# A recommender's CIN layer on one core: weights gathered in two halves, from the input and from a smaller table

## The chip, the cores and the metric

The kernel runs on one core of one Trainium2 chip. The metric is the device time of one execution in microseconds (us). A profile of one execution goes with it. In it PE is TensorE (matmuls; PEld are its weight loads), DVE is VectorE, ACT is ScalarE, POOL is GpSimd and SP is SyncE. "L391" is line 391 of the kernel. A fp32 matmul leaves two records, so 8 records of line 391 are 4 matmuls.

## The reference

Three layers combine an embedding `X0` of 1024 rows, 39 fields and 64 elements with itself; each is summed over the elements, and a last linear layer takes the 192 sums to one number for each row:

```python
F, E, HID = 39, 64, [64, 64, 64]
def _cin_layer(Xk, X0, W, b):
    O = W.shape[0]
    Hk, Fdim = (Xk.shape[1], X0.shape[1])
    Wr = W.reshape(O, Hk, Fdim)
    return jnp.einsum('bhe,bfe,ohf->boe', Xk, X0, Wr) + b[None, :, None]
Xk = X0; outs = []
for W, b in ((W0, b0), (W1, b1), (W2, b2)):
    Xk = _cin_layer(Xk, X0, W, b)
    outs.append(Xk.sum(axis=-1))
return jnp.concatenate(outs, axis=-1) @ fc_w.T + fc_b
```

All data are fp32. The last layer only enters through its sum, so the kernel folds fc into W2 (a vector v), and v into W1: a table T[b, a, h]. What is left for each pair of fields is one product of two embeddings, a weight from W0 for the first layer's output x1, and a weight from T for a second output z; the answer is the sum over x1 * (z + fc) and a linear part.

## The kernel before

A start-up of some 33 us makes the table and gathers weights. Then come 32 blocks of 32 rows. For a block, four "rolled" tiles `r` (the 39 fields in four orders, gathered by GpSimd from a copy `xd` of the input) give six products `p` of 128 field pairs each (chunks 0 to 5), and for each pair of blocks the tiles `u` and `v` give one more product for the rest (chunk 6, half the rows for each block). TensorE multiplies each product with that chunk's weights `wa`. The weights of both orders of a pair, (a, b) and (b, a), are gathered into `wa` and `wb` and added.

The table has x1's half (W0) and z's half (T) side by side, 512 bytes a row; unused pairs point at a row of zeros:

```python
NONE = FT * FT - 1                     # FT = F + 1 = 40
table = dram.tile([FT * FT, 2 * H], F32, name="table")
...                                    # start-up: loads and memsets
load(0, nc.gpsimd)
nc.gpsimd.memset(w0s, 0.0); nc.gpsimd.memset(w0r, 0.0)     # (two lines)
load(1, nc.gpsimd)
...
halves(w2s, w2); halves(w1s, w1)                            # SyncE's queue
nc.scalar.dma_start(fc, fc_w.rearrange("o (l h) -> h (o l)", h=H))
load_ones(0, nc.scalar)
nc.scalar.copy(warm, warm)
for k in range(2):
    nc.scalar.dma_start(w0s[H * k : H * k + F], w0t[:, NA * k : NA * (k + 1), :])
nc.scalar.dma_start(w0r[0:F], w0t[:, 2 * NA : F, :])
for s in range(2):
    nc.scalar.copy(fc2[H * s : H * s + H, 0:1], fc[:, 2:3])
    nc.scalar.copy(v2[H * s : H * s + H, F:FT], fc[:, 1:2])
...                                    # VectorE works out the lists of indices
roll(0, (0, 1, 2))
roll(1, (0, 1))
...                                    # pv matmuls (fc into W2), transposes, v2; more lists
...                                    # pt and pr matmuls (v into W1)
spin(9)                                # filler matmuls on zeros
for s, copy in enumerate((nc.vector.tensor_copy, nc.scalar.copy)):
    ...                                # PSUM to part and rest
nc.sync.dma_start(tablev[:, 0:NA, :], part[0:FT])
nc.scalar.dma_start(tablev[:, NA : 2 * NA, :], part[H : H + FT])
nc.sync.dma_start(tablev[:, 2 * NA : FT, :], rest[0:FT])

def weights(c):                        # two gathers of 128 rows of 512 bytes
    for k, w in enumerate((wa, wb)):
        nc.gpsimd.indirect_dma_start(
            w[:, c], None, table[:], bass.IndirectOffsetOnAxis(ap=wlists[:, k, c : c + 1], axis=0)
        )

weights(0); weights(1); weights(3)     # (one call a line in the kernel)
roll(1, (2,))
weights(2)
roll(0, (3,))
weights(4); weights(5)
roll_half(0)                           # u and v
weights(6)
roll(1, (3,))
load(2); load(3)
```

The main loop, and the order of its steps:

```python
PAIRS = ((0, 1), (0, 2), (0, 3), (1, 2), (2, 3), (1, 3)); ORDER = (0, 1, 3, 2, 4, 5)
steps = [(n, c) for n in range(2) for c in ORDER[:3]]
steps += [(0, c) for c in ORDER[3:] + (NPAIR,)] + [(1, c) for c in ORDER[3:]]
for n in range(2, NBLK, 2):
    steps += [(n, c) for c in ORDER + (NPAIR,)] + [(n + 1, c) for c in ORDER]
...
p = {s: product(*s) for s in steps[:2]}
add(steps[0][1])
p[steps[2]] = product(*steps[2])
add(steps[1][1]); add(steps[2][1])     # (one a line)
p[steps[3]] = product(*steps[3])
for at, (n, c) in enumerate(steps[:-TAIL]):
    if c == 0 and n + 4 < NBLK:
        load(n + 4)
    add(steps[at + 2][1])              # VectorE: wa += wb, once for each chunk
    multiply(n, c, p.pop((n, c)))      # TensorE: 4 matmuls (8 half-height ones for chunk 6)
    if at - 1 in over:
        finish(over[at - 1]); fields(over[at - 1] + 1)
    if at + AHEAD < len(steps):        # AHEAD = 4
        n, c = steps[at + AHEAD]
        p[n, c] = product(n, c)        # VectorE
        if c == ORDER[-1] and n + 2 < NBLK:
            roll(n + 2)
            ...                        # and u, v of the next pair of blocks
```

There are four buffers for `p`.

Of the kernel before, what the change touches and what calls it, by code (L numbers as in the profile page):

```python
# [49 lines left out]
F32 = mybir.dt.float32  # L52
I32 = mybir.dt.int32
AF = mybir.ActivationFunctionType
ALU = mybir.AluOpType
# [3 lines left out]
FH = F * H  # L59
# [20 lines left out]
FT = F + 1  # L80
NONE = FT * FT - 1
NTAB = 3
# [13 lines left out]
def cin_kernel(ctx: ExitStack, tc: tile.TileContext, x, w0t, b0, w1, b1, w2, b2, fc_w, fc_b, out):  # L96
# [16 lines left out]
    def load(n, engine=nc.sync):  # L113
        first = n % 2 * FT
        engine.dma_start(
            xd[n // 2 % NTAB][first : first + F].rearrange("f (b e) -> f b e", e=E),
            xv[:, n * BB : (n + 1) * BB, :],
        )
# [7 lines left out]
    def roll(n, tiles=range(4)):  # L126
        for i in tiles:
            gather_rows(rt[n % 2][:, i], n, n % 2 * 4 + i)
# [20 lines left out]

    table = dram.tile([FT * FT, 2 * H], F32, name="table")  # L150
    tablev = table.rearrange("(b a) h -> b a h", a=FT)

    prep = tc.tile_pool(name="prep", bufs=1)
    with prep as prep:
        w2s = prep.tile([128, FH // 2], F32, name="w2s")
        w1s = prep.tile([128, FH // 2], F32, name="w1s")
        fc2 = prep.tile([128, 32], F32, name="fc2")
        ones = prep.tile([16, 128], F32, name="ones")
        zeros = prep.tile([128, MM], F32, name="zeros")
        w0s = prep.tile([128, NA * H], F32, name="w0s")  # L160
        w0r = prep.tile([H, NR * H], F32, name="w0r")
        part = prep.tile([128, NA, 2 * H], F32, name="part")
        rest = prep.tile([H, NR + 1, 2 * H], F32, name="rest")
        place = prep.tile([128, 1], I32, name="place")
        warm = prep.tile([1, 1], F32, name="warm")


        nc.gpsimd.iota(place, pattern=[[0, 1]], base=0, channel_multiplier=1)
        nc.vector.memset(warm, 0.0)
        nc.vector.memset(zeros, 0.0)  # L170
        nc.vector.memset(fc2, 0.0)  # L171
        nc.vector.memset(ones, 1.0)
        load(0, nc.gpsimd)
        nc.gpsimd.memset(w0s, 0.0)
        nc.gpsimd.memset(w0r, 0.0)
        load(1, nc.gpsimd)
        nc.gpsimd.memset(v2, 0.0)
        nc.gpsimd.memset(rest[:, NR], 0.0)

        def halves(dst, w):  # L180
            for s in range(2):
                nc.sync.dma_start(
                    dst[H * s : H * s + H], w[:, s * (FH // 2) : (s + 1) * (FH // 2)]
                )

        def load_ones(k, engine):
            for row in (F, FT + F):
                engine.dma_start(xd[k][row].rearrange("(p c) -> p c", c=128), ones)

        halves(w2s, w2)  # L190
        halves(w1s, w1)
        nc.scalar.dma_start(fc, fc_w.rearrange("o (l h) -> h (o l)", h=H))
        load_ones(0, nc.scalar)
        nc.scalar.copy(warm, warm)
        for k in range(2):
            nc.scalar.dma_start(w0s[H * k : H * k + F], w0t[:, NA * k : NA * (k + 1), :])
        nc.scalar.dma_start(w0r[0:F], w0t[:, 2 * NA : F, :])
        for s in range(2):
            nc.scalar.copy(fc2[H * s : H * s + H, 0:1], fc[:, 2:3])  # L199
            nc.scalar.copy(v2[H * s : H * s + H, F:FT], fc[:, 1:2])  # L200
# [52 lines left out]
        nc.vector.tensor_scalar(lists[:, 4:8], fields_of[:, 0:4], float(FT), None, ALU.add)  # L253
        roll(0, (0, 1, 2))
        roll(1, (0, 1))

        step(row, HR, 1.0, half)
        fused(q, half, -float(HR), row, ALU.mult, ALU.add)
        nc.vector.tensor_tensor(field[4], q, step(q, F, -float(F)), ALU.add)
        nc.vector.tensor_tensor(field[4], field[4], step(q, 56, 11.0), ALU.add)  # L260
        nc.vector.tensor_scalar(field[5], q, float(F), None, ALU.min)
        fused(t, q, -50.0, step(q, 45, 1.0), ALU.add, ALU.mult)
        for y in (t, step(q, 50, -float(F)), step(q, 56, -6.0)):
            nc.vector.tensor_tensor(field[5], field[5], y, ALU.add)

        nc.vector.tensor_scalar(half, half, float(FT), None, ALU.mult)
        nc.vector.tensor_scalar(lists[:, 8:10], fields_of[:, 4:6], half, None, ALU.add)

# [5 lines left out]
        for k in range(2):  # L274
            for u in range(4):
                rows = slice(u % 2 * H, u % 2 * H + H)
                f0 = u // 2 * 19 + k * 10
                nc.tensor.matmul(  # L278
                    pv[k][32 * u : 32 * u + 32, 0:320],
                    fc2[rows],  # L280
                    w2v[rows, f0 : f0 + 10, :],
                    start=True,
                    stop=True,
                )
# [9 lines left out]
        nc.scalar.copy(v2[H:128, 0:F], column)  # L294
        nc.scalar.copy(part[:, :, H : 2 * H], w0s.rearrange("b (a h) -> b a h", h=H))
        nc.scalar.copy(rest[:, 0:NR, H : 2 * H], w0r.rearrange("b (a h) -> b a h", h=H))


        nc.vector.tensor_scalar(scaled, fields_of, float(FT), None, ALU.mult)
        pair = prep.tile([128, 4], F32, name="pair")  # L300
        nc.vector.tensor_scalar(wlists[:, 0, 0:3], scaled[:, 1:4], field[0], None, ALU.add)
        nc.vector.tensor_scalar(wlists[:, 1, 0:3], fields_of[:, 1:4], scaled[:, 0:1], None, ALU.add)
        nc.vector.tensor_tensor(wlists[:, 0, 3:5], scaled[:, 2:4], fields_of[:, 1:3], ALU.add)
        nc.vector.tensor_tensor(wlists[:, 1, 3:5], scaled[:, 1:3], fields_of[:, 2:4], ALU.add)
        for m, (i, k) in enumerate(((1, 3), (3, 1), (4, 5), (5, 4))):
            nc.vector.tensor_tensor(pair[:, m : m + 1], scaled[:, k : k + 1], field[i], ALU.add)
        fused(wlists[:, 0, 5:6], extra, float(NONE), pair[:, 0:1], ALU.mult, ALU.max)
        fused(wlists[:, 1, 5:6], extra, float(NONE), pair[:, 1:2], ALU.mult, ALU.max)
        last = step(q, 62, float(NONE))
        nc.vector.tensor_tensor(wlists[:, 0, 6:7], pair[:, 2:3], last, ALU.max)  # L310
        nc.vector.tensor_scalar(t, q, float(F), float(NONE), ALU.is_lt, ALU.mult)
        nc.vector.tensor_tensor(pair[:, 3:4], pair[:, 3:4], t, ALU.max)
        nc.vector.tensor_tensor(wlists[:, 1, 6:7], pair[:, 3:4], last, ALU.max)

# [14 lines left out]
        for s in range(2):  # L329
# [3 lines left out]
            )  # L333
        spin(9)
        for s, copy in enumerate((nc.vector.tensor_copy, nc.scalar.copy)):
            at = slice(32 * s, 32 * s + 32)
            copy(part[:, :, at], pt[s].rearrange("b (a h) -> b a h", h=32))
            copy(
                rest[:, 0:NR, at],
                pr[s][H * s : H * s + H, 0 : 32 * NR].rearrange("b (a h) -> b a h", h=32),  # L340
            )
        nc.sync.dma_start(tablev[:, 0:NA, :], part[0:FT])
        nc.scalar.dma_start(tablev[:, NA : 2 * NA, :], part[H : H + FT])
        nc.sync.dma_start(tablev[:, 2 * NA : FT, :], rest[0:FT])
        for k in range(1, NTAB):
            load_ones(k, nc.scalar)


    def weights(c):
        for k, w in enumerate((wa, wb)):  # L350
            nc.gpsimd.indirect_dma_start(  # L351
                w[:, c], None, table[:], bass.IndirectOffsetOnAxis(ap=wlists[:, k, c : c + 1], axis=0)
            )

    weights(0)
    weights(1)
    weights(3)
    roll(1, (2,))
    weights(2)
    roll(0, (3,))  # L360
    weights(4)
    weights(5)
    roll_half(0)
    weights(6)
    roll(1, (3,))
# [16 lines left out]
    def multiply(n, c, p, quarters=range(BLK // MM)):  # L382
        half = c == NPAIR
        for k in (n, n + 1) if half else (n,):
            if k not in po:
                po[k] = [bank("po") for _ in range(BLK // MM)]
        for m in quarters:

            for h in range(2 if half else 1):
                w = slice(h * HR, (h + 1) * HR) if half else slice(0, 128)  # L390
                nc.tensor.matmul(  # L391
                    po[n + h][m],
                    wa[w, c, :],
                    p[w, bass.ts(m, MM)],
                    start=c == opens[n + h],
                    stop=c == closes[n + h],
                )
# [47 lines left out]

    def add(c):
        nc.vector.tensor_tensor(wa[:, c], wa[:, c], wb[:, c], ALU.add)

    AHEAD = 4
# [14 lines left out]
    last_weights()  # L464
    p = {s: product(*s) for s in steps[:2]}
    added = set()
# [6 lines left out]
    add(steps[0][1])  # L473
    p[steps[2]] = product(*steps[2])
    add(steps[1][1])
    add(steps[2][1])
    p[steps[3]] = product(*steps[3])
    fields(0)
# [76 lines left out]
```

## Time and profile before

| what | value |
|---|---|
| time, median of 3 runs | 767.87 us (766.59 to 769.39) |
| profiled span | 766.5 us, mean TensorE clock 0.991 |
| main matmuls, first start | 33.13 us |
| W2 and W1 issued on SyncE's queue | 0.74 and 1.99 us |
| first matmul on W2 (pv) | 9.77 us |
| last table issue | 17.49 us |
| first gather from the table | 28.36 us |

The page gives each engine's busy time as a share of the span; a line of the waits reads "engine, line <- releaser: us in all, times, the longest". A line of the timeline reads start, duration, engine, line, operation, output <- inputs with shapes, how many were merged, and in brackets the idle time ahead of it and what ended it. A gather's duration on POOL is that of its issue; the data land later. A wait for several events is put down to the one that came last.

### The profile page before, as it was taken

The numbers are of one execution on the slowest core, as the hardware profiler recorded it, in microseconds if no ns is written. First come the engines' busy times: TensorE is split into PE (matmuls) and PEld (weight loads), VectorE is DVE, ScalarE is ACT, GpSimd is POOL, SyncE is SP. The second block draws the span as 40 slices with busy tenths as digits, with TensorE's granted clock in tenths as the row PEclk, the third lists the DMA queues.
The fourth block names the chain that finished last, engine by engine and source line by source line (L and its number), as shares of the span: only waits on it lengthen the run. The fifth ranks groups of instructions, "written<-read, shape, count | busy, mean of one in ns | idle before, by whom it ended". The sixth has DMA issues, their size and how long they took to land.

```text
span 766.5 us, 5146 instructions
## 1 busy us (share of the span) xinstructions
PE 745.1 (97%) x1856; PEld 322.3 (42%) x1856; DVE 641.2 (84%) x479; ACT 160.4 (21%) x207; POOL 320.4 (42%) x185
## 2 busy tenths in 40 slices
PE   6597999999999999999999999999999999999998
PEld 2243444444444444444444444444444444444443
DVE  5375988889888889888889988888988888998885
ACT  2002312122221212222121222112122221112212
POOL 4487273542436244253634325363442636334200
PEclk9899999999999999999999999999999999999999
DMA  8849958576865757676575777657577764737400
GB/s 260 268 151 384 402 183 342 168 273 231 327 240 203 283 170 276 244 316 241 189 287 183 276 254 292 256 178 284 185 297 252 267 260 147 284 150 317 165 0 0
DMA packets 62839, 181.79 MB, mean 237 GB/s; under 512 B 41364, under 2 KB 41499, under 8 KB 42254
## 3 DMA queue, kind: packets, MB, share of 16 engines
q0 software_dynamic: 23712, 169.34, 57.5%
q1 hardware_dynamic: 38494, 11.36, 6.4%
q10 hardware_dynamic: 608, 0.77, 0.3%
q8 instruction: 14, 0.23, 0.1%
q14 instruction: 11, 0.09, 0.0%
HBM read 180.58 MB, written 11.10 MB: 250 GB/s over the span
## 4 chain that ended last, share of the span: by engine, by line
PE 91%; DMA 3%; issue 2%; POOL 2%; DVE 1%; ACT 0%; DVEq 0%; POOLq 0%; SPq 0%
PE po L391 91%; DMA table<-rest 1%; POOL wa L351 1%; DMA u<-xd,lists 1%; POOL wb L351 1%; DMA wb<-table,wlists 0%; PE pt L322 0%; DVE blocks L289 0%; POOL r L122 0%; DVE fields_of L233 0%; DVE tmp L229 0%; DVE tmp L233 0%; PE pr L331 0%; DVE g L430 0%; DVE sums L432 0%
## 5 line engine op out<-in xcount | busy, mean ns | idle before, releaser
L391 PE MATMUL po<-p,wa 128*128 128x512 f32 (+1 forms) x1792 | 724.3, 597 | 11.9 <-DVE wa L471 11.9
L377 DVE TENSOR_TENSOR p<-r 128x2048 f32<-128x2048 f32 x192 | 434.5, 2291 | 88.1 <-PE po L391 82.2
L391 PEld LDWEIGHTS po<-p,wa 128*128 128x128 f32 (+1 forms) x1792 | 315.0, 190 | 420.4 <-issue 395.4
L122 POOL DMA_INDIRECT r<-xd,lists x128 | 249.3, 1948 | 366.0 <-DVE p L377 340.0
L410 ACT ACTIVATE x<-po,b0s 64x512 f32<-64x512 f32 x124 | 84.5, 684 | 356.4 <-PE po L391 349.8
L404 ACT COPY g<-u 39x1024 f32<-39x1024 f32 x64 | 66.6, 1043 | 216.2 <-DVE sums L421 181.2
L416 DVE SCALAR_TENSOR_TENSOR g<-po,fc,x 64x512 f32<-64x512 f32 x124 | 86.4, 734 | 0.0
L421 DVE TENSOR_REDUCE sums<-g 103x16 f32<-103x1024 f32 x62 | 75.6, 1220 | 2.2
L379 DVE TENSOR_TENSOR p<-u,v 128x2048 f32<-128x2048 f32 x16 | 36.5, 2284 | 9.1 <-DMA v<-xd,lists 9.1
L122 POOL DMA_INDIRECT u<-xd,lists x16 | 29.8, 1859 | 4.9 <-issue 4.6
L122 POOL DMA_INDIRECT v<-xd,lists x16 | 16.6, 1035 | 4.9 <-issue 4.9
L351 POOL DMA_INDIRECT wa<-table,wlists x7 | 11.0, 1573 | 14.6 <-DMA table<-rest 12.8
L211 PE MATMUL idle<-zeros 128*128 128x512 f32 x24 | 12.9, 686 | 1.5 <-DVE fc L171 1.5
L471 DVE TENSOR_TENSOR wa<-wa,wb 128x128 f32<-128x128 f32 x7 | 2.0, 291 | 11.6 <-DMA wb<-table,wlists 11.6
L351 POOL DMA_INDIRECT wb<-table,wlists x7 | 9.7, 1382 | 2.1 <-issue 2.1
L211 PEld LDWEIGHTS idle<-zeros 128*128 128x128 f32 x24 | 4.8, 212 | 8.2 <-issue 6.8
L430 DVE SCALAR_TENSOR_TENSOR g<-po,fc,x1q 64x512 f32<-64x512 f32 x4 | 3.0, 742 | 5.3 <-ACT x1q L429 5.3
L278 PE MATMUL pv<-w2s,fc 64*32 64x320 f32 x16 | 2.8, 764 | 4.5 <-ACT fc L199 4.5
L289 DVE STREAM_TRANSPOSE blocks<-pv 64x320 f32<-64x320 f32 x4 | 2.1, 514 | 3.7 <-issue 3.6
L429 ACT ACTIVATE x1q<-po,b0s 64x512 f32<-64x512 f32 x4 | 2.7, 684 | 10.2 <-PE po L391 10.2
L278 PEld LDWEIGHTS pv<-w2s,fc 64*32 64x32 f32 x16 | 1.0, 142 | 6.7 <-ACT fc L199 6.1
L432 DVE TENSOR_REDUCE sums<-g 103x8 f32<-103x512 f32 x4 | 2.7, 686 | 0.1
(74 smaller groups left out, 30.0 us busy)
## 6 DMA issues: line engine op xcount, KB each, us to landing
xd<-in_x SPq DMA_DIRECT2D x30, 312.0 KB
r<-xd,lists POOLq DMA_INDIRECT x128
w2s<-in_w SPq DMA_DIRECT2D x2, 312.0 KB
xd<-in_x POOLq DMA_DIRECT2D x2, 312.0 KB
w1s<-in_w SPq DMA_DIRECT2D x2, 312.0 KB
table<-part SPq DMA_DIRECT2D x1, 320.0 KB
table<-part ACTq DMA_DIRECT2D x1, 320.0 KB
w0s<-in_w0t ACTq DMA_DIRECT2D x2, 156.0 KB
```

The source lines that it names most:

```text
L122: nc.gpsimd.indirect_dma_start(dst, None, table, bass.IndirectOffsetOnAxis(ap=lists[:, k : k + 1], axis=0))
L211: nc.tensor.matmul(idle, zeros[:, 0:128], zeros, start=True, stop=True)
L278: nc.tensor.matmul(pv[k][32 * u : 32 * u + 32, 0:320], fc2[rows], w2v[rows, f0 : f0 + 10, :], start=True, stop=True,)
L351: nc.gpsimd.indirect_dma_start(w[:, c], None, table[:], bass.IndirectOffsetOnAxis(ap=wlists[:, k, c : c + 1], axis=0))
L377: nc.vector.tensor_tensor(p, rt[n % 2][:, i], rt[n % 2][:, k], ALU.mult)
L379: nc.vector.tensor_tensor(p, ut[n // 2 % 2], vt[n // 2 % 2], ALU.mult)
L391: nc.tensor.matmul(po[n + h][m], wa[w, c, :], p[w, bass.ts(m, MM)], start=c == opens[n + h], stop=c == closes[n + h],)
L404: nc.scalar.copy(gt[H : H + F], ut[n // 2 % 2][h : h + F, bass.ts(m, SUB)])
L410: nc.scalar.activation(x1[m // 2][:, bass.ts(m % 2, MM)], po[n][m][H:128], AF.Identity, bias=b0s[H:128])
L416: nc.vector.scalar_tensor_tensor(gt[0:H, at], po[n][m][0:H], fc[:, 0:1], x1[m // 2][:, at], ALU.add, ALU.mult)
L421: nc.vector.tensor_reduce(sums[:, b_at : b_at + SB], gt.rearrange("p (b e) -> p b e", e=E), AX.X, ALU.add)
L430: nc.vector.scalar_tensor_tensor(gt[0:H], po[n][m][0:H], fc[:, 0:1], t, ALU.add, ALU.mult)
```

## The change

W0's half of the weights is no longer copied into the table: it is gathered from the input itself. The table keeps T alone, with rows of 256 bytes. Each chunk now takes four gathers of 128 rows of 256 bytes instead of two of 512. Rows beyond the source are skipped instead of pointing at zeros, so `wa` and `wb` are cleared first. W2 is loaded first and as one transfer, with fc's column going straight to where pv's matmuls read it. Two of block 0's tiles are issued ahead of the table's way through the engines and a third just ahead of the table's gathers; block 1's load and tiles come after the first table gathers. The purpose is to have the table, and with it the first main matmul, earlier, and to use GpSimd while it waits for the table.

The core of the diff (cut at "..."):

```diff
-NONE = FT * FT - 1
+NONE = 4096
...
-    table = dram.tile([FT * FT, 2 * H], F32, name="table")
-    tablev = table.rearrange("(b a) h -> b a h", a=FT)
+    table = dram.tile([FT * F, H], F32, name="table")
+    tablev = table.rearrange("(b a) h -> b a h", a=F)
+
+    def weights(c, into, of, last):
+        for k in range(2):
+            nc.gpsimd.indirect_dma_start(
+                (wa, wb)[k][:, c, into : into + H],
+                None,
+                of,
+                bass.IndirectOffsetOnAxis(ap=wlists[:, k, c : c + 1], axis=0),
+                bounds_check=last,
+                oob_is_err=False,
+            )
+
+    def weights_x1(c):
+        weights(c, H, w0t.rearrange("b a h -> (b a) h"), F * F - 1)
+
+    def weights_z(c):
+        weights(c, 0, table[:], FT * F - 1)
...
+        for t in (wa, wb):
+            nc.gpsimd.memset(t, 0.0)
...
-        load(0, nc.gpsimd)
-        nc.gpsimd.memset(w0s, 0.0)
-        nc.gpsimd.memset(w0r, 0.0)
-        load(1, nc.gpsimd)
...
-        halves(w2s, w2)
-        halves(w1s, w1)
-        nc.scalar.dma_start(fc, fc_w.rearrange("o (l h) -> h (o l)", h=H))
+        fcv = fc_w.rearrange("o (l h) -> h (o l)", h=H)
+        nc.sync.dma_start(w2s, w2.rearrange("o (s n) -> (o s) n", s=2))
+        for s in range(2):
+            nc.scalar.dma_start(fc2[s:128:2, 32 * s : 32 * s + 1], fcv[:, 2:3])
+        load(0)
+        nc.scalar.dma_start(fc, fcv)
+        nc.sync.dma_start(w1s[0:H], w1[:, 0 : FH // 2])
         load_ones(0, nc.scalar)
+        nc.scalar.dma_start(w1s[H:128], w1[:, FH // 2 : FH])
         nc.scalar.copy(warm, warm)
-        for k in range(2):
-            nc.scalar.dma_start(w0s[H * k : H * k + F], w0t[:, NA * k : NA * (k + 1), :])
-        nc.scalar.dma_start(w0r[0:F], w0t[:, 2 * NA : F, :])
...
-        roll(0, (0, 1, 2))
-        roll(1, (0, 1))
...                                      # (some index arithmetic moves ahead, some behind the table)
+        weights_x1(0)
+        roll(0, (0,))
+        weights_x1(1)
+        roll(0, (1,))
...                                      # (pv's matmuls: all 128 rows of W2 at once)
+        weights_x1(3)
...
-        spin(9)
+        spin(13)
...
-    weights(0)
-    weights(1)
-    weights(3)
-    roll(1, (2,))
-    weights(2)
+    roll(0, (2,))
+    weights_z(0)
+    weights_z(1)
+    load(1, nc.gpsimd)
+    weights_z(3)
+    roll(1, (0, 1, 2))
+    weights_x1(2)
+    weights_z(2)
     roll(0, (3,))
-    weights(4)
-    weights(5)
+    weights_x1(4)
+    weights_z(4)
     roll_half(0)
-    weights(6)
+    weights_x1(5)
+    weights_z(5)
+    weights_x1(6)
+    weights_z(6)
     roll(1, (3,))
...
-    p = {s: product(*s) for s in steps[:2]}
+    p = {steps[0]: product(*steps[0])}
...
     add(steps[0][1])
-    p[steps[2]] = product(*steps[2])
-    add(steps[1][1])
-    add(steps[2][1])
-    p[steps[3]] = product(*steps[3])
+    for k in (1, 2, 3):
+        p[steps[k]] = product(*steps[k])
+        if k < 3:
+            add(steps[k][1])
```

## The prediction

> **What bounds the kernel now.** I read the page's engine list first, then the waits, then the chain, then the first 75 us of the timeline engine by engine.
>
> ```profile
> PE 745.1 (97%) x1856; PEld 322.3 (42%) x1856; DVE 641.2 (84%) x479; ACT 160.4 (21%) x207; POOL 320.4 (42%) x185
> ```
>
> TensorE is the bound over the whole run. The waits say where it is not fed:
>
> ```profile
> PE po L391 <- DVE wa L471: 11.9, 2, 7.8
> PE pv L278 <- ACT fc L199: 4.5, 1, 4.5
> ```
>
> So the main loop waits twice, both times for a weight sum (the add of line 471). The TensorE timeline dates them:
>
> ```profile
> 33.13 29.25 PE L391 MATMUL po<-p,wa 128*128 128x512 f32 x64 [7.85 <-DVE wa L471]
> 66.44 9.03 PE L391 MATMUL po<-p,wa 128*128 128x512 f32 x24 [4.06 <-DVE wa L471]
> ```
>
> Eight steps (8 records each) run from 33.13, then there is a hole, and from 66.44 on there is no further wait. A warm step lasts 3.43 us (records start 0.429 us apart). Step 8 starts at 66.44, step 9 at 71.77, step 10 at 75.41 us, and from there the kernel needs 766.5 - 75.4 = 691.1 us, which the change leaves alone. So the whole question is: **when does step 10 start?** (Steps counted from 0, in the order of the list `steps`: step 8 is block 0 with weight chunk 5, step 9 the half-height chunk 6, step 10 block 1 with chunk 2.)
>
> What sets it is GpSimd, which issues every gather. From its timeline after the table has landed:
>
> ```profile
> 28.36 0.95 POOL L351 DMA_INDIRECT wa<-table,wlists  x1 [12.75 <-DMA table<-rest]
> 29.62 0.95 POOL L351 DMA_INDIRECT wb<-table,wlists  x1 [0.30 <-issue]
> ...
> 43.70 2.67 POOL L351 DMA_INDIRECT wa<-table,wlists  x1 [0.31 <-issue]
> 46.67 1.89 POOL L351 DMA_INDIRECT wb<-table,wlists  x1 [0.30 <-issue]
> 48.87 1.92 POOL L351 DMA_INDIRECT wa<-table,wlists  x1 [0.30 <-issue]
> 51.09 1.90 POOL L351 DMA_INDIRECT wb<-table,wlists  x1 [0.30 <-issue]
> ...
> 59.46 0.94 POOL L122 DMA_INDIRECT r<-xd,lists  x1 [0.31 <-issue]
> ```
>
> and VectorE at the same time:
>
> ```profile
> 43.26 8.92 DVE L377 TENSOR_TENSOR p<-r 128x2048 f32<-128x2048 f32 x4 [1.93 <-DMA r<-xd,lists]
> ...
> 63.89 2.29 DVE L379 TENSOR_TENSOR p<-u,v 128x2048 f32<-128x2048 f32 x1 [9.12 <-DMA v<-xd,lists]
> 66.10 0.28 DVE L471 TENSOR_TENSOR wa<-wa,wb 128x128 f32<-128x128 f32 x1
> 67.91 2.29 DVE L377 TENSOR_TENSOR p<-r 128x2048 f32<-128x2048 f32 x1 [1.52 <-DMA r<-xd,lists]
> 70.12 0.28 DVE L471 TENSOR_TENSOR wa<-wa,wb 128x128 f32<-128x128 f32 x1
> ```
>
> The reader is to see three things. An issue costs 0.95 us and 0.30 us of gap, 1.25 us, whether its rows have 512 or 8192 bytes. When it starts while VectorE multiplies it lasts about 2 us: it ends some 0.85 us after that product does. And VectorE is in order: the product of u and v stands ahead of the add for chunk 5, the product with block 1's field tile 3 ahead of the add for chunk 6, so TensorE's "wait for wa" is really a wait for v and for that tile, the last of GpSimd's list.
>
> **What the Trainium skill says.** "SBUF — State Buffer", section "SBUF: two separate sides", describes the lock: a DMA issued from GpSimd needs descriptors written by GpSimd, which cannot get at the shared port pair while certain VectorE instructions hold it. The trace agrees: 2.67, 1.89, 1.92, 1.90 us against 0.95. "DMA: Bandwidth & Descriptors", section "Anatomy of one DMA — SWDGE (gpsimd) path", gives a fixed cost of about 2 us per transfer, so splitting one gather in two saves nothing per piece. Here a weight gather issued at 36.30 was added at 38.82, 2.5 us, for 64 KB. "TensorE: Matmul & The Clock Gate", section "What's actually happening", says that an idle window of about 3.4 us halves the clock. Here the first records after both holes start about 0.86 us apart instead of 0.43; step 8 took 5.33 us, 1.9 more than a warm one.
>
> **The change part by part.** (1) The start. The copies of W0 through SBUF (on ScalarE) go, and W2's transfer is first and alone, with fc's column brought straight into place. TensorE's first useful matmul (pv) waited until 9.77 us for ScalarE's copy of fc, which stood behind the W0 transfers; I estimate 6 us. From there to the last table issue it was 17.76 - 9.77 = 8 us, so about 14 us. The table write then needed 10.15 us in the chain, behind five 1 MB gathers (DMA share near 1.0 from 5 to 25 us). Now only two 1 MB gathers are ahead, and the table is half as large: I estimate 4 us, landing at 18.
>
> (2) GpSimd ahead of the table. The lists are ready at about 6.5 us (5.8 before, plus five small VectorE operations). Six W0 gathers and three 1 MB gathers, 9 x 1.25, take it to 17.8. So the first table gather starts at about 18.5 instead of 28.36, and the first main matmul at about 24.5 instead of 33.13: 8.6 us **early**. The 13 filler matmuls (11.1 us, from about 13) end at the same time, so that TensorE is warm here, worth another 1.7 us. If nothing followed, this would give 757 to 759 us.
>
> (3) GpSimd behind it. Before, from the table's landing to block 1's tile 3, it issued 19 gathers: 14 of weights, 3 field tiles, u and v, from 28.36 to 60.40, 32.0 us. Of that 19 x 1.25 = 23.8, and 8.3 us are seven stretched issues, 1.2 us each. After, the same stretch has 14 table gathers, 8 of W0 (chunks 2, 4, 5, 6), the load of block 1, five field tiles (block 1's tiles 0 and 1, which went ahead of the table before, are now behind), u and v: **30 issues**. 30 x 1.25 = 37.5, and ten products fall into the stretch, 10 x 1.2 = 12: 49.5 us, so it ends at 68.0. Walked issue by issue, with each issue that starts in a product held to 0.87 us past its end, it ends nearer 70; the same walk on the old order gives step 9 at 71.5 and step 10 at 75.0, where the trace has 71.77 and 75.41. So 68 to 70 against 60.40.
>
> (4) What TensorE sees. v is issue 21 of the 30: 21 x 1.25 + 8 x 1.2 + 18.5 = 54.4 (57 in the walk), landing some 6.5 later, so step 8 starts at 64 to 66, about where it did. Then tile 3 of block 1: issued by 68 to 70, 4.8 us to its product (38.50 to 43.26 for its like), 2.29 of product, 0.3 of add: 75.4 to 77.7 for step 9, against 71.77. The hole ahead of it is near 8 us, so step 9 runs at half clock for 3.4 us, 1.7 more, and step 10 starts at 75.4 + 5.3 = 80.7 to 77.7 + 5.3 = 83.0, against 75.41: **5.3 to 7.6 us later**. The early start is eaten on the way: block 1's first product waits for its tiles until about 42.
>
> **The rivals.** Rival A: the early start survives (757 to 761). The filler count, raised from 9 to 13, looks like a start meant for 24 us. Against it: in the windows of 40:50 and 50:60 us GpSimd was already busy 8.7 and 8.2 of 10 us with half as many weight gathers. It could still come true in part if gathers of 256 bytes with skipped rows issue faster: at 0.85 instead of 0.95 us the walk puts step 10 at 79.1, 3.7 late; at 0.6 the two would about cancel. Rival B: the bounds test makes an issue dearer. No row of the old trace has such a gather. At 1.3 us the walk puts step 10 at 87, 779.6 in all. Rival C: the table is late after all, since transfers from SyncE's queue sat 3.7 us between issue and first packet when the queues were full; each microsecond past 18.5 is then a microsecond on the end, 2 to 3 us in all.
>
> **Range and chances.** The middle of the sum is 6.5 us on 767.87: 774.5. The low end, 764, is rival A by half; the high end, 782, is B or C. For 2% faster, 752.5, the whole start would have to be gained twice over. For 2% slower, 783.2, both B and C would have to hold, or a new hole open.
>
> **What would show it.** Right: first main matmul at 24 to 25 us; a second hole of several microseconds right ahead of the half-height step; GpSimd busy over 8 of 10 us from 20 to 70 us with issues of about 2 us beside products; step 10 past 80 us; no holes later. Wrong: table gathers of clearly less than 0.9 us or more than 1.1; products that no longer stretch them; step 10 at 75 or earlier; or any wait of TensorE beyond 90 us, which I take to be none.

## The result and the profile after

The changed kernel takes 776.5 us (median of 4 runs, 774.03 to 777.43), the kernel before 767.83 beside it: a ratio of 1.0107, 95% interval 1.0077 to 1.0137. The change costs some 8.7 us.

The page's engine list of the changed kernel (busy time, share of the span, instructions):

```profile
PE 751.8 (97%) x1864; PEld 324.1 (42%) x1864; DVE 641.5 (83%) x482; ACT 158.7 (20%) x203; POOL 338.4 (44%) x196
```

and its waits of TensorE:

```profile
PE po L406 <- DVE wa L483: 11.0, 3, 7.9
PE po L406 <- DVE p L392: 6.8, 1, 6.8
```

GpSimd works 18 us longer. The wait of pv for ScalarE has gone. TensorE in the main loop waited 11.9 us in all before, and now 17.8: 6.8 us for a product are new. The TensorE timeline dates the waits (start, duration, engine, line, operation, tiles, records; in brackets the idle time ahead):

```profile
5.17 3.65 PE L282 MATMUL pv<-w2s,fc 128*32 128x320 f32 x16
...
26.89 10.88 PE L406 MATMUL po<-p,wa 128*128 128x512 f32 x24 [1.34 <-DVE wa L483]
44.60 19.79 PE L406 MATMUL po<-p,wa 128*128 128x512 f32 x40 [6.83 <-DVE p L392]
66.18 3.70 PE L406 MATMUL po<-p,wa 128*128 128x512 f32 x8 [1.79 <-DVE wa L483]
77.75 22.62 PE L406 MATMUL po<-p,wa 64*128 64x512 f32 x53 [7.87 <-DVE wa L483]
```

The early start is there: 26.89 us instead of 33.13. It is gone at step 3, which starts at 44.60, about where it did before. Step 8 starts at 66.18 (before 66.44), step 9, the half-height one, at 77.75 (71.77), and step 10, read from the single records, at 84.22 (75.41). From there to the end it is 775.7 - 84.22 = 691.5 us, as before (691.1). So 8.8 of the 9.2 us between the two profiled spans are there when step 10 starts, and **all of them arise between step 8 and step 10**. Of the 8.8 us, 6.0 are the later start of step 9, and 2.8 are its length: it took 6.47 us where it took 3.64 before, at half clock after the hole.

Why step 9 is late is read from VectorE's timeline, back from its add:

```profile
22.58 2.29 DVE L392 TENSOR_TENSOR p<-r 128x2048 f32<-128x2048 f32 x1 [5.01 <-DMA r<-xd,lists]
26.50 0.29 DVE L483 TENSOR_TENSOR wa<-wa,wb 128x128 f32<-128x128 f32 x1 [1.63 <-DMA wb<-table,wlists]
...
42.26 2.29 DVE L392 TENSOR_TENSOR p<-r 128x2048 f32<-128x2048 f32 x1 [8.24 <-DMA r<-xd,lists]
...
63.63 2.29 DVE L394 TENSOR_TENSOR p<-u,v 128x2048 f32<-128x2048 f32 x1 [7.01 <-DMA v<-xd,lists]
65.84 0.28 DVE L483 TENSOR_TENSOR wa<-wa,wb 128x128 f32<-128x128 f32 x1
75.20 2.29 DVE L392 TENSOR_TENSOR p<-r 128x2048 f32<-128x2048 f32 x1 [9.08 <-DMA r<-xd,lists]
77.41 0.28 DVE L483 TENSOR_TENSOR wa<-wa,wb 128x128 f32<-128x128 f32 x1
```

TensorE waits for `wa`, but the 0.28 us add at 77.41 stands behind a product that waited 9.08 us for a field tile. GpSimd's timeline has that tile's issue (a POOL duration is that of the issue):

```profile
14.20 0.96 POOL L123 DMA_INDIRECT r<-xd,lists  x1 [0.30 <-issue]
...
19.33 0.99 POOL L156 DMA_INDIRECT wa<-table,wlists  x1 [0.31 <-issue]
20.63 1.00 POOL L156 DMA_INDIRECT wb<-table,wlists  x1 [0.30 <-issue]
...
23.23 2.51 POOL L156 DMA_INDIRECT wb<-table,wlists  x1 [0.30 <-issue]
...
48.40 1.90 POOL L156 DMA_INDIRECT wa<-table,wlists  x1 [0.30 <-issue]
...
57.56 1.01 POOL L156 DMA_INDIRECT wa<-in_w0t,wlists  x1 [0.30 <-issue]
...
64.09 2.70 POOL L156 DMA_INDIRECT wb<-in_w0t,wlists  x1 [0.30 <-DMA wb<-in_w0t,wlists]
...
69.70 0.96 POOL L123 DMA_INDIRECT r<-xd,lists  x1 [0.30 <-issue]
```

(In this profile `in_w0t` is W0 as it lies in the input.) Block 1's tile 3 is issued at 69.70 (before 59.46), and its product begins 5.5 us later. Nearly every gap in this list is 0.30 us: **GpSimd never stops between the table's landing and that tile**. The first table gather came 9.0 us earlier (19.33 against 28.36), but 30 issues follow where there were 19, and ten of them are stretched by a product beside them (1.86 to 2.83 us instead of 1.00) where there were seven. It used 51.3 us instead of 32.0: 19.3 more against 9.0 gained, and so it ends 10.3 later.

### The profile page after: what moved, and what is told of

Its sections match the earlier page's. It is cut to its first block, busy times and chain, and to the rows that moved or that the text cites. A ratio compares the mean times of both kernels' runs of the same rounds, so it can differ in the third digit from the quotient of the medians.

```text
span 775.7 us, 5206 instructions
## 1 busy us (share of the span) xinstructions
PE 751.8 (97%) x1864; PEld 324.1 (42%) x1864; DVE 641.5 (83%) x482; ACT 158.7 (20%) x203; POOL 338.4 (44%) x196
## 4 chain that ended last, share of the span: by engine, by line
PE 90%; DMA 4%; issue 3%; POOL 3%; DVE 0%; ACT 0%; POOLq 0%; DVEq 0%
PE po L406 89%; DMA r<-xd,lists 2%; POOL wa L156 1%; DMA w1s<-in_w 1%; POOL wb L156 1%; DMA wb<-in_w0t,wlists 1%; DMA table<-part 0%; DMA w2s<-in_w 0%; POOL v L123 0%; PE pt L311 0%; POOL r L123 0%; POOL u L123 0%; POOL xd L116 0%; PE pr L320 0%; DVE g L445 0%
## 5 line engine op out<-in xcount | busy, mean ns | idle before, releaser
L220 PE MATMUL idle<-zeros 128*128 128x512 f32 x32 | 16.2, 659 | 1.5 <-DVE zeros L189 1.5
L156 POOL DMA_INDIRECT wa<-in_w0t,wlists x7 | 8.7, 1243 | 6.8 <-DVE wlists L268 5.0
L156 POOL DMA_INDIRECT wb<-in_w0t,wlists x7 | 10.1, 1444 | 2.1 <-issue 1.5
L220 PEld LDWEIGHTS idle<-zeros 128*128 128x128 f32 x32 | 6.3, 206 | 10.2 <-issue 8.7
L444 ACT ACTIVATE x1q<-po,b0s 64x512 f32<-64x512 f32 x4 | 2.7, 684 | 10.2 <-PE po L406 10.2
L282 PE MATMUL pv<-w2s,fc 128*32 128x320 f32 x16 | 3.6, 763 | 0.0
L311 PE MATMUL pt<-w1s,v 64*64 64x512 f32 x8 | 2.2, 1107 | 1.0 <-DMA w1s<-in_w 1.0
```

Of the source, the lines that this page charges most:

```text
L156: nc.gpsimd.indirect_dma_start((wa, wb)[k][:, c, into : into + H], None, of, bass.IndirectOffsetOnAxis(ap=wlists[:, k, c : c + 1], axis=0) ...
L220: nc.tensor.matmul(idle, zeros[:, 0:128], zeros, start=True, stop=True)
L282: nc.tensor.matmul(pv[k][32 * u : 32 * u + 32, 0:320], fc2[:, u % 2 * 32 : u % 2 * 32 + 32], w2v[:, f0 : f0 + 10, :], start=True, stop=True,)
```

## The experiments

**The theory:** the end is set by GpSimd's list up to block 1's tile 3; the late W0 gathers lengthen it, the stretch by VectorE's products multiplies them, and the earlier start of the main loop is worth nothing while that tile is the last to come. **Rivals:** the half-clock periods cost the time, the bounds test makes issues dear, or the start itself went wrong (table or tile 1 late), so that more was to be had there.

All twelve runs, each against the kernel before, run beside it on the same chip. "Step 10" is the start of that step's first matmul in the profiled execution. That is one execution for each run, within some 1.6 us of the run's median, but 3.5 us above it in e6a; the two of the changed kernel differ by 0.9 us, so smaller differences in this column say little:

| run | median us | ratio (95% interval) | step 10 |
|---|---|---|---|
| before | 767.83 | 1 | 75.41 |
| after | 776.5 | 1.0107 (1.0077 to 1.0137) | 84.22 |
| after_again | 776.98 | 1.0117 (1.0090 to 1.0144) | 85.15 |
| e1_no_late_w0 | 763.75 | 0.9955 (0.9940 to 0.9971) | 72.44 |
| e2_tile3_first | 771.44 | 1.0054 (1.0034 to 1.0073) | 78.09 |
| e3_no_bounds_test | 774.15 | 1.0093 (1.0062 to 1.0125) | 82.82 |
| e5_scalar_products | 765.70 | 0.9975 (0.9963 to 0.9987) | 72.36 |
| e4a_start_alone_5 | 764.43 | 0.9936 (0.9912 to 0.9960) | 71.69 |
| e4b_start_alone_3 | 766.52 | 0.9972 (0.9957 to 0.9987) | 74.96 |
| e6a_start_5_load_early | 766.11 | 0.9980 (0.9968 to 0.9992) | 76.85 |
| e6b_start_3_load_late | 767.46 | 0.9998 (0.9983 to 1.0013) | 73.94 |
| e8_two_tiles_one_table | 763.54 | 0.9945 (0.9930 to 0.9959) | 68.19 |
| f1_loads_late | 765.03 | 0.9976 (0.9964 to 0.9987) | 72.40 |
| f2_after_loads_late | 775.79 | 1.0111 (1.0078 to 1.0143) | 83.89 |

### The late W0 gathers, left out

e1_no_late_w0 is the changed kernel without the eight W0 gathers behind the table. It leaves out the first layer's weights of four chunks, which stay zero; all matmuls and products are done.

```diff
     roll(1, (0, 1, 2))
-    weights_x1(2)
     weights_z(2)
     roll(0, (3,))
-    weights_x1(4)
     weights_z(4)
     roll_half(0)
-    weights_x1(5)
     weights_z(5)
-    weights_x1(6)
     weights_z(6)
     roll(1, (3,))
```

> The changed kernel without its eight W0 gathers behind the table (chunks 2, 4, 5, 6; the first layer's half of these weights stays zero). Theory (GpSimd's count of issues sets the second hole): 22 issues instead of 30 behind the table's landing, so block 1's tile 3 is issued by about 60 us instead of 70.7, step 9 starts near 67 us instead of 77.75, step 10 near 70.6 instead of 84.2, and the time falls by 11 to 14 us, to 762 to 766. Rival (the transfers themselves, or the queues of the DMA engines, are late): eight gathers of 32 KB are 0.26 MB of some 8 MB, so the time moves by under 2 us.

Measured: 763.75 us, within what the theory gave. GpSimd's timeline and TensorE's, from 27 us on:

```profile
58.65 0.96 POOL L123 DMA_INDIRECT r<-xd,lists  x1 [0.30 <-issue]
```

```profile
45.65 24.72 PE L402 MATMUL po<-p,wa 128*128 128x512 f32 x54 [6.61 <-DVE p L388]
```

Tile 3 is issued 11 us earlier than in the changed kernel, and the hole ahead of the half-height step is gone: from 45.65 us on TensorE does not wait. The hole ahead of step 3 stays (6.61 us), so that one is not made by the late W0 gathers. From the first table gather (20.62, here 1.3 us later) to the end of tile 3's issue GpSimd needs 39.0 us instead of 51.3. Eight gathers with their stretches are thus worth some 12 us, more than the change's whole loss, although nine of the 22 issues left are still stretched.

### The same gathers, block 1's tile 3 ahead of the last eight

```diff
     weights_z(4)
     roll_half(0)
+    roll(1, (3,))
     weights_x1(5)
     weights_z(5)
     weights_x1(6)
     weights_z(6)
-    roll(1, (3,))
```

> The changed kernel with block 1's tile 3 issued right behind u and v, ahead of the last eight weight gathers; nothing else moves. Theory (the product of step 10 stands ahead of chunk 6's sum on VectorE and waits for a tile that is last in GpSimd's list): the wait moves from the tile to chunk 6's own last gather, step 9 starts near 74.5 us, the hole ahead of it shrinks from 7.9 to about 3 us and its half-clock stretch with it: step 10 near 78 instead of 84.2, time down by 5 to 7 us. Rival (only the number of issues counts, in whatever order): no change, within 1 us.

Measured: 771.44 us, 4 to 5 less than the changed kernel (5.1 by the medians, 4.1 by the ratios), at or just under the 5 to 7 expected. Only the place of one issue differs. TensorE's timeline, then VectorE's:

```profile
67.06 3.70 PE L406 MATMUL po<-p,wa 128*128 128x512 f32 x8 [3.06 <-DVE wa L483]
...
74.46 1.13 PE L406 MATMUL po<-p,wa 64*128 64x512 f32 x4 [3.69 <-DVE wa L483]
```

```profile
66.93 2.28 DVE L392 TENSOR_TENSOR p<-r 128x2048 f32<-128x2048 f32 x1
74.11 0.29 DVE L483 TENSOR_TENSOR wa<-wa,wb 128x128 f32<-128x128 f32 x1 [4.90 <-DMA wb<-table,wlists]
```

The product no longer waits; the add now waits by itself for the last weights, which come 3.3 us earlier than the tile did. It shows both halves of the reading: the wait named `wa` was the tile's, and behind it stands the next item of the same GpSimd list. The hole falls from 7.87 to 3.69 us, step 9 takes 3.63 us at full clock instead of 6.47, and step 10 comes 6.1 us earlier. So the half clock of the changed kernel goes with its hole; it is a consequence of the wait, not a cause beside it.

### The bounds test

e3_no_bounds_test drops the test and holds the indices to the last row that all sources have. It leaves the skipping of unused rows out: they are read, so those weights are not zero.

```diff
                 bass.IndirectOffsetOnAxis(ap=wlists[:, k, c : c + 1], axis=0),
-                bounds_check=last,
-                oob_is_err=False,
...
-        nc.vector.tensor_scalar(wlists[:, 1, 0:3], fields_of[:, 1:4], scaled[:, 0:1], None, ALU.add)
+        nc.vector.tensor_scalar(wlists[:, 1, 0:3], fields_of[:, 1:4], scaled[:, 0:1], 1520.0, ALU.add, ALU.min)
...                                              # (the other lists likewise)
```

> The changed kernel with indices held to row 1520 and no bounds test on the gathers, so that unused rows are read instead of skipped (their weights are not zero then). Theory (the count of issues, not the test, is what costs): an issue falls from 1.00 to 0.95 us, 28 times 0.05 or 1.4 us at most, and about half of it is lost in issues that wait for products: time down by 0 to 1.5 us. Rival (skipping rows is what makes the weight gathers slow): issues well under 0.95 us and 5 us or more gained.

Measured: 774.15 us, 2.4 less by the medians and 1.1 by the ratios; the two intervals overlap, so no gain in time is resolved. The issues themselves are resolved. In GpSimd's timeline the changed kernel has 1.01 for this gather:

```profile
57.41 0.95 POOL L156 DMA_INDIRECT wa<-in_w0t,wlists  x1 [0.30 <-issue]
```

The test costs some 0.06 us an issue. By the 22 weight gathers behind the table's landing that is 1.3 us, and step 10 is 1.4 us earlier in this profile. The test may be about 1 of the 8.7 us; it is not what made the loss.

### VectorE's products, taken away beside GpSimd's list

e5_scalar_products leaves out the multiplications of the first eleven steps: ScalarE copies the later tile instead, and VectorE only copies one element of it, so that it still waits in the same places.

```diff
+        if (n, c) in steps[:11]:
+            nc.scalar.copy(p, rt[n % 2][:, PAIRS[c][1]] if c < NPAIR else vt[n // 2 % 2])
+            nc.vector.tensor_copy(seen, p[0:1, 0:1])
+            return p
...                                              # (fields(0) moved behind the seventh step)
```

> The changed kernel with the products of its first eleven steps replaced by copies of the later of the two tiles on ScalarE (the multiplication is left out), each read by a one-element VectorE copy so that VectorE's order and waits stay. Theory (ten issues are stretched by VectorE's two-input products, about 1.2 us each): no issue behind the table lasts over 1.2 us, block 1's tile 3 is issued near 58 to 60 us instead of 70.7, step 9 starts near 65 to 67, time down by 10 to 14 us. Rival (the stretched issues wait for something else, such as the ring of descriptors or earlier landings): they stay near 2 us and the time within 2 us.

Measured: 765.7 us, 10 to 11 less than the changed kernel with every gather in place. GpSimd's timeline:

```profile
43.38 0.99 POOL L156 DMA_INDIRECT wa<-table,wlists  x1 [0.30 <-issue]
...
59.03 0.96 POOL L123 DMA_INDIRECT r<-xd,lists  x1 [0.30 <-issue]
```

No issue between the table and tile 3 lasts over 1.2 us, and tile 3 comes 10.7 us earlier. So the stretch is tied to VectorE's products and is the other part of the loss: **the eight gathers and the ten stretches each cost more than the change gained, and taking away either one turns the loss into a small gain**. The two do not add up, since each of e1 and e5 ends where other waits take over.

### The start alone, on the old list

e4a_start_alone_5 and e4b_start_alone_3 take the kernel before, with its table of 512-byte rows and its 14 weight gathers, and give it the change's start: W2 first in one transfer, fc's column direct, block 0's load on SyncE, 13 fillers. They also take over the change's order of the first products and adds (each add right behind its product), as do e6a, e6b, e8 and f1; what that alone is worth was not tried. Five or three field tiles stand ahead of the table.

```diff
-        halves(w2s, w2)
-        halves(w1s, w1)
+        nc.sync.dma_start(w2s, w2.rearrange("o (s n) -> (o s) n", s=2))
+        for s in range(2):
+            nc.scalar.dma_start(fc2[s:128:2, 32 * s : 32 * s + 1], fcv[:, 2:3])
+        load(0)
...                                              # (fc, W1's halves, and load(1) last on SyncE)
-        spin(9)
+        spin(13)
...
         roll(0, (0, 1, 2))
-        roll(1, (0, 1))                          # e4b alone
...
-    roll(1, (2,))
+    roll(1, (0, 1, 2))                           # e4b alone
...                                              # (the first products and adds as in the change)
```

> The kernel before with the change's start alone: W2 first and as one transfer, fc's column straight into place, block 0's load on SyncE's queue, 13 fillers. Weights stay in rows of 512 bytes in one table, five tiles ahead of it as before. Theory (the start is a gain, the split of the gathers is the loss): W0's copies now lie behind W1, pv starts near 5.2 us instead of 9.77, the table is issued near 14 and lands at 20 to 23 us under five 1 MB gathers; 19 issues follow, 32 us as before, step 9 starts at 64 to 68 instead of 71.77, time 4 to 8 us under before: 760 to 764. Rival (the start brings nothing because the five gathers hold the table up until they are through, near 27 us): within 2 us of before.

> As the start alone, but with three tiles ahead of the table and block 1's tiles 0 and 1 behind the first three chunks' weights, as in the change. Theory: the table lands at 18 to 20 us, 21 issues follow; first main matmul near 24, a hole ahead of step 3 as in the changed kernel (step 3 near 41), step 9 at 62 to 64, time 7 to 11 us under before: 757 to 761. Rival (tiles behind the table cost what the earlier table brings): no better than the start alone with five tiles ahead.

Measured: 764.43 us for five tiles, inside its range, and 766.52 for three, a miss. The TensorE timeline of e4a from 30 to 70 us:

```profile
34.63 35.84 PE L387 MATMUL po<-p,wa 128*128 128x512 f32 x82 [7.78 <-issue]
```

This start is 1.5 us *later* than in the kernel before, and the kernel is still 4 us faster: once started, TensorE does not wait at all. It is the plainest sign that the first matmul's time is not what counts. GpSimd's list agrees: v was issued at 52.23 us (before 55.70) and block 1's tile 3 at 57.88 (59.46), so the hole of 4.06 us ahead of step 8 did not open. But my reason for e4a's gain was wrong: its table was not early (first gather from it at 26.55). Block 1's load, put last on SyncE, stood in the way: the issue of the table's first part behind it took 4.60 us, against 0.29 in the changed kernel, and block 1's first tile was issued only at 24.06.

Two runs moved that load, to GpSimd's start (e6a) and behind the second pair of weight gathers (e6b):

```diff
-        load(1)                                  # both
+        load(1, nc.gpsimd)                       # e6a: with the memsets at the start
...
     weights(1)
+    load(1, nc.gpsimd)                           # e6b
     weights(3)
```

> The start alone with five tiles, but block 1's load goes on GpSimd's queue near 4 us, as in the kernel before, instead of on SyncE's queue ahead of the table, where it held up both the table and block 1's tiles. Theory (the load in the table's queue cost about 4 us): the table lands near 22 to 24 us although five 1 MB gathers are ahead of it, the first weight gather starts there instead of at 26.55, step 10 at 68 to 70 instead of 71.69, time 760 to 763. Rival (the five gathers hold up the table, not the load): first weight gather at 26 or later, time as the start alone with five tiles, 764.

> The start alone with three tiles, block 1's load on GpSimd's queue behind the first table gathers, as in the changed kernel, so that nothing stands ahead of the table in its queue. Theory: the table lands near 19 to 20 us instead of 25.7, 22 issues follow it (30 in the changed kernel), first main matmul near 25, step 10 near 69 to 71, time 760 to 763, some 14 us under the changed kernel with the same start: what is left of the difference is the split of the gathers. Rival (the larger table, 512-byte rows, is what lands late): first table gather past 23 us, time 764 or more.

Measured: 766.11 and 767.46 us. Both missed, and what the rivals said of the first gather from the table held: it began at 27.99 and 24.66 us (the first from a profile 3.5 us above e6a's median). By the ratios e6a is even slower than e4a, though the load no longer stood in SyncE's queue. In GpSimd's timeline of e6b, where three tiles are all that stands ahead:

```profile
24.66 0.95 POOL L345 DMA_INDIRECT wa<-table,wlists  x1 [12.73 <-DMA table<-rest]
```

GpSimd is idle for 12.73 us, and its first gather from the table comes 5.3 us later than in the changed kernel. A 512-byte table behind three tiles in a row is late; the start alone is not what made the changed kernel's table early.

### A version that beats both

e8_two_tiles_one_table keeps one 512-byte table (14 weight gathers, no late W0) and puts two tiles and block 1's load ahead of it:

```diff
-        roll(0, (0, 1, 2))
-        roll(1, (0, 1))
+        roll(0, (0, 1))
+        load(1, nc.gpsimd)
...
     weights(0)
+    roll(0, (2,))
     weights(1)
     weights(3)
-    roll(1, (2,))
+    roll(1, (0, 1, 2))
     weights(2)
     roll(0, (3,))
     weights(4)
-    weights(5)
     roll_half(0)
-    weights(6)
+    weights(5)
     roll(1, (3,))
+    weights(6)
```

> One table of 512-byte rows as before, with the change's start, and the lesson of the runs so far: two tiles and block 1's load ahead of the table, tile 2 behind chunk 0's weights, block 1's tile 3 ahead of chunk 6's weights. Theory (the gathers in flight hold up the table; behind it the number of issues counts): the table lands near 20 to 21 us instead of 24.66 with three tiles ahead, 22 issues follow, first main matmul at 24 to 26, step 10 near 67 to 70 instead of 75.4 before and 84.2 in the changed kernel, time 758 to 762, the best of all. Rival (the larger table lands late whatever is ahead of it): first table gather past 23 us, time 763 or more.

Measured: 763.54 us, 4.6 less than the kernel before beside it (768.09): the shortest median of all the kernels that compute everything, and by its ratio level with e4a. That misses 758 to 762 and is what the rival said, time and table: the first gather from the table came at 23.09. Its TensorE timeline from 28 to 100 us:

```profile
28.97 5.26 PE L387 MATMUL po<-p,wa 128*128 128x512 f32 x8 [3.00 <-DVE wa L467]
35.84 7.13 PE L387 MATMUL po<-p,wa 128*128 128x512 f32 x16 [1.61 <-DVE wa L467]
43.55 49.04 PE L387 MATMUL po<-p,wa 128*128 128x512 f32 x120 [0.57 <-DVE p L373]
93.75 6.70 PE L387 MATMUL po<-p,wa 128*128 128x512 f32 x15 [1.16 <-DVE p L373]
```

The holes are small, and step 10 starts at 68.19, 7.2 us ahead of before, inside the 67 to 70 expected. Of these, 5.8 us reach the end of the profiled execution (which was 1.1 us below the median): TensorE is now so early that it meets a later wait for a product, 1.16 us at 93.75.

Two last runs held the loads of blocks 2 to 5 back until the first weight sum, on the thought that they delayed the table and tile 1: f1 in e8, f2 in the changed kernel.

```diff
     add(steps[0][1])
+    mark = dram.tile([1, 1], F32, name="mark")
+    nc.sync.dma_start(mark, wa[0:1, steps[0][1], 0:1])
+    load(2)
+    load(3)
...                                              # (their calls behind the last gather are gone)
```

> The one-table kernel with two tiles ahead, its loads of blocks 2 to 5 (1.3 MB in 256-byte packets, issued right behind the table) held until the first weight sum is made. Theory (these loads share the DMA engines with block 0's tile 2 and block 1's tiles, which landed some 7 us after their issue): those tiles land about 2 us earlier, step 3 starts near 41.5 instead of 43.55, time 1 to 3 us lower: 760.5 to 762.5. Rival (the tiles wait for their own queue): step 3 as before, time within 1 us of 763.5.

> The changed kernel with the same four loads held until the first weight sum. Theory (the loads delayed tile 1 of block 0, which landed 8 us after its issue, and with it the first product, a stretched issue and the first main matmul): first main matmul near 24.5 instead of 26.9, but GpSimd's 30 issues still end near 69 to 70.5, so the time falls by 2 us at most: 774.5 to 776.5. Rival (whatever brings the first matmul forward brings the end forward): 772.5 to 774.5.

f1 missed: 765.03 us. Its first main matmul came 1.3 us earlier (27.66), but step 3 came 2.7 us later (46.27), and the time is 1.5 us more than e8's by the medians, 2.4 by the ratios. The loads had not been what delayed block 1's tiles: the product of its tiles 0 and 1 began 7.1 us after the end of tile 1's issue in e8 (34.06 to 41.20) and in f1 (36.78 to 43.93). That issue ended 2.7 us later because products, now earlier, stood beside it and the one ahead of it (2.09 and 2.21 us instead of 0.94).

f2's time is where the theory had it: 775.79 us, with an interval that overlaps the changed kernel's. Its TensorE timeline:

```profile
25.75 7.11 PE L403 MATMUL po<-p,wa 128*128 128x512 f32 x16 [0.95 <-DVE wa L480]
...
77.26 3.79 PE L403 MATMUL po<-p,wa 64*128 64x512 f32 x8 [9.29 <-DVE wa L480]
```

The first matmul is 1.1 us earlier, the half-height step 0.5, and the hole ahead of it is longer by 1.4 us: what is gained at the start is waited for later. But the first product came at 22.20 instead of 22.58, so the theory was wrong about tile 1: the loads did not hold it.

> The changed kernel beside the one above on the same chip: 774 to 777.5 us, ratio to before 1.008 to 1.013, step 10 near 84 us, as in its first runs.

The changed kernel, run once more beside e8, took 776.98 us (1.0117), as at first: the loss repeats.

## Why the prediction was right, and where its terms were off

**The start (step 1)** went nearly as written: pv's matmuls at 5.17 us (predicted 6), the last table issue from 14.28 to 14.56 (14), the last tile ahead of the table gathers issued at 18.07 with the table there (18). In the chain of waits the write took

```profile
13.99 3.81 DMA table<-part
```

where I had 4 from before's 10.15. The estimate came out for this order of issues and this table; e6b and e8 show that it does not carry over to others.

**GpSimd ahead of the table (step 2)** began later: the list was written at 6.60, but the first gather started at 7.54, and the six of its nine issues that have the test took 1.30 or more each instead of 1.25. First table gather 19.33 against 18.5. The first main matmul came at 26.89, not 24.5: **this term was mis-sized by 2.4 us**. I had counted six microseconds from the first table gather to TensorE, without the tiles ahead of it in GpSimd's queue. The first add, at 26.50, waited for chunk 0's second table gather. That one was issued at 20.63 with no stretch, but landed 5.8 us later, at 26.4: right behind the packets of tile 2, which was issued ahead of it at 18.07 and moved its last 8192-byte packet at 25.67. In f2, which holds the loads of blocks 2 to 5 back, tile 2 landed at 24.9, the gather at 25.2, and the add began at 25.36. So the gather's data seem to come in behind tile 2, which stands just ahead of the table's gathers, and the loads account for some 1.1 us of the 2.4; tile 2 alone was not moved to try it. Tile 1 was late as well: its issue ended at 15.16, and it was used at 22.58, 7.4 us later against the 4.8 I took elsewhere. Its packets ran beside the table's own; what held it stays open. By the argument of steps 3 and 4 this error costs nothing, and f2 bears that out.

**GpSimd behind the table (step 3)** was the argument, and it held: 30 issues, exactly ten stretched, by 12.9 us in all (predicted 12), tile 3's issue ending at 70.66 (predicted 68 to 70). The stretch itself is a two-input TENSOR_TENSOR of VectorE against the issue of an indirect gather: 1.86 to 2.83 us beside it, at most 1.11 in e5 without it. Here I read the page too broadly when I wrote that the trace agrees: "SBUF — State Buffer" of the Trainium skill, section "SBUF: two separate sides", has the lock for VectorE's two-port modes, which a copy can enter and a tensor_tensor cannot, and reports that a tensor_tensor did not stall a DMA. It also has an instruction with two SBUF inputs contend with a GpSimd instruction that reads SBUF; whether the reading of the gather's index list is such a case was not tried. These gathers were stalled, and the measurement decides. e1 and e5 took the two factors away one at a time: the hole ahead of step 9, 7.87 us, was gone in e1, and in e5's TensorE timeline it is 2.20, for a copy on ScalarE:

```profile
67.03 53.20 PE L412 MATMUL po<-p,wa 64*128 64x512 f32 x134 [2.20 <-ACT p L393]
```

**What TensorE sees (step 4):** step 8 at 66.18 (64 to 66), step 9 at 77.75 (75.4 to 77.7), both just past the upper edge. Step 9 then took 6.47 us where I had 5.3. I had assumed half clock for 3.4 us, 1.7 more. The windows of the changed kernel show it for longer (bounds, length, busy time and count of PE, PEld, DVE, ACT and POOL, then the granted clock, the DMA share and GB/s):

```profile
73.30:83.50 10.20, 5.75 (x14) 2.55 (x16) 6.90 (x4) 1.60 (x3) 8.51 (x6) 0.50 0.97 368
```

The clock fell to half inside the hole and stayed there for 10.2 us, of which about 5.7 had TensorE at work. "TensorE: Matmul & The Clock Gate" of the Trainium skill, section "What's actually happening", gave me a window of 3.4 us; its page also has the window free-running, and 10.2 is three of them. The other half-clock stretch of this trace, 42.55 to 49.37, is two, and ends 4.8 us after step 3 began. In both the clock came back only after a whole window of work (80.1 to 83.5, where work had begun at 77.75, and 46.0 to 49.4, where it had begun at 44.60), so a better estimate from the same page would have been 3.4 to 6.8 us of half clock after the hole, not 3.4. So step 10 began at 84.22 instead of 80.7 to 83.0, 2.4 us behind the middle of that range: 1.2 us are step 9's later start and 1.2 its slower run. They account for the 2 us by which 774.5 was short of 776.5. The 691.1 us behind it held (691.5).

**The rivals.** A, an early start that survives, failed: gathers of 256 bytes took 1.00 us, no less than those of 512, and the two holes ate the start. B, a dear bounds test, failed at its size: 0.06 us an issue, not 0.3. C, a late table, was not seen in the changed kernel but in e4a, e4b, e6a, e6b and e8 (first gather at 23.09 to 27.99). Later holes, which would have made me wrong, did not open.

## What to carry to other kernels

Work moved off one engine's path can lengthen another's: count the instructions on the engine that hands out the last buffer, multiply by what one really costs there (here 1.3 us, and 2.6 beside a product), and compare that with what the start gains. Splitting a gather in two doubles its issues whatever its size. And ask of every wait which entry of an in-order queue it truly stands for: the "wait for wa" was a wait for a field tile, and moving that tile's one issue forward won back 4 to 5 of the 8.7 us.

## What the runs showed of the hardware that I had not expected

- With gathers of 8192-byte rows in flight from GpSimd, a write in SyncE's queue began late. In the changed kernel the tiles stand between small W0 gathers, and the table's packets begin at 14.81, 1.1 us after its first issue at 13.74. In e8, with two tiles and a load in a row, the first issue was at 14.28 and the first packet at 17.54, 3.3 us later; the last packet ended at 21.7 instead of 17.7. Of these 4.0 us 0.5 are the later issue, 2.2 the longer wait and 1.2 the transfer of a table of twice the size; wait and size were not tried apart. In e8 the gathers' packets were through when the write began, but in e6b (first packet at 17.68) and in the kernel before (20.63) they ran on until 22.7 and 29.3, so it does not wait for all of them. "DMA: Bandwidth & Descriptors" of the Trainium skill, section "Queues, rings and completion order", has each engine go round-robin over the queues, a packet at a time; from that I had not expected so long a wait for the first packet, and its cause was not tried.
- Half clock came in stretches of 6.8 and 10.2 us, ending 4.8 and 5.75 us after TensorE was back at work. The length of the hole did not decide whether it came: in e2 holes of 3.06 and 3.69 us left the clock full, in e5 one of 2.20 us was followed by 3.4 us of half clock.
- The bounds test costs 0.06 us a gather (1.00 against 0.94), and skipping rows saved nothing at the issue.
